# Folding the third hop's weights into the first in a four-layer graph network

## The chip, the cores and the metric

The kernel runs on one core of one Trainium2 chip. The time is that of the device for one execution, in microseconds (us); several runs are taken, and the median is compared. One further execution is recorded by the hardware profiler; its span, from the first to the last recorded instruction, is a little shorter than its time.

The engines are called PE (TensorE, the matrix unit), DVE (VectorE), ACT (ScalarE), POOL (GpSimd) and SP (the sync engine, which here issues nearly all loads). Each works through its own instructions in program order.

## The reference

There are 3327 nodes with 64 features and one weighted adjacency matrix `adj` (3327 x 3327, sparse in content, stored dense, fp32). Four layers follow each other, each with a layernorm and a relu ahead and a residual behind:

```python
h = relu(layernorm(x)); x = x + gated(h)     # 2 gated cells: m = adj @ (h W); GRU-like gates; relu
h = relu(layernorm(x)); x = x + ranked(h)    # w = decay ** rank of each nonzero in its row (last 100); w @ (h W) + b
h = relu(layernorm(x)); x = x + squared(h)   # three times: z = (adj * adj) @ z;  z = z @ W.T + b
h = relu(layernorm(x)); x = x + two_hop(h)   # twice: x = tanh([adj @ x, x] @ W[k])
```

So the adjacency is multiplied eight times with a 3327 x 64 matrix, the eight *hops* 0 to 7. Hops 3, 4 and 5 belong to the third layer. With `S = adj * adj` it computes

```
z1 = S h  W0' + b0;   z2 = S z1 W1' + b1;   z3 = S z2 W2' + b2;   x = x + z3
```

where the multiplication by `S` from the left and by a weight from the right may be done in any order.

## The kernel before

**Data.** The nodes are padded to 3328 = 26 blocks of 128. The node features `xs` stay in on-chip memory as 13 positions x 2 halves `s`. Their outputs are made in four *chunks*: chunks 0, 1 and 2 of three positions (384 columns per half), chunk 3 of four (512). Chunks 0 and 1 are group 0, chunks 2 and 3 group 1 (`GROUPS`). A matmul of a hop (`propagate`, L613) takes the node rows `y[k]` of one block as weights and one adjacency tile as moving data, and adds into an accumulator bank per chunk; half `s` of the columns goes to one half of the array's columns. So a sum holds features on partitions (two halves of 64) and nodes along the row. [...] Each tile (128 rows, one group's columns) is loaded by SP into one of 20 slots and is used by hop k and, some units later, by hop k+1.

**Order.** `units` lists (hop, chunk, tile) in the order of the calls at L1044 to L1052: a pass alone for hop 0 of group 0, then joint passes, in which group 1 does hops 0 and 1, group 0 hops 1 and 2, group 1 hops 2 and 3, and so on, the last alone for hop 7 of group 0. In a joint pass the tiles whose source nodes belong to the other group come first; the tiles of the group's own nodes come last, chunk by chunk, so that a chunk's sum ends before the next chunk's last eight tiles (`sweep=8`). Hop k+1 of the pass then asks for the node rows that hop k has just produced, first those of one chunk, then those of the other. The program is laid out by hand: the order in which Python emits instructions is each engine's order. `run` (L717) goes through the units; it emits loads ahead, masks, squares (`square`, L444: ACT, and every third on DVE when no side work is open), the expansion for hop 2 (`expand`, L490), and the matmuls.

**Side work.** What follows a chunk's sum is a generator, `after_0` to `after_7`, begun when the last matmul of that sum is emitted. Each `yield us` puts off its next part until so many nominal microseconds of streaming matmuls have been emitted (`spend`; 0.86 for 512 columns). So a task's parts are strewn among the other instructions, and its parts on DVE stand in one row with those of the other tasks.

**The pieces concerned.**

- `fold_hops` (L228), some 165 us in, multiplies hop 3's and hop 4's weights of the third layer together, so that hop 3 applies W0W1 at once and hop 4 only adds b1. `product(i, j)` puts `bd[i] bd[j]` into `bd[i]`; `bd[:, 1]`, `[:, 2]` and `[:, 3]` are W0, W1 and W2. `brow` holds biases as rows, `hopcol` as columns.
- `after_3` (L991) evacuates hop 3's sum, multiplies it by the weights on PE (`dense_to_nodes`: this matmul turns features into nodes as well) and adds a bias row on DVE.
- `after_4` (L1003) uses `sums_to_nodes` (L813): ACT copies the sum out of the accumulator with a bias per feature, and DVE turns it into node rows by sixteen 32 x 32-block transposes (L825).
- `after_5` (L1006) evacuates (`evacuate`: DVE for even chunks, L761, ACT for odd), multiplies by W2 on PE, adds the result to `xs` on DVE (`residual`, L865), takes layernorm and relu (L843 to L858, the power of -1/2 on POOL at L854), hands over the rows `y[6]`, and later turns them into features by `transpose_on_vector` (L809, sixteen transposes). b2 was added to `xs` at the end of `after_2` (`add_row`, L871).
- `gru` (L874) ends in cell 0 with two relus, the first half on DVE, the second on ACT; `after_0` (L947) then turns both halves into node rows, for group 1 by DVE transposes (L961).
- `last_sources(g)` (L564) builds the weights of each row's last entry, needed at the end of hop 2: POOL clears half a slot (L570), SP loads two pieces (L574), DVE computes (L576, L580), ACT writes `lastw` (L582), and the slot half is freed, which masks (`make_mask`, L472 and the POOL load L477) may take next.
- `after_7` (L1029) ends with the last residual on DVE (L1037) and the output DMA of the chunk (L1039). For the last hop chunk 1 is split into parts 4 (two positions) and 5 (one), so the outputs come as chunks 2, 3, 0, 4, 5.

Of the kernel before, what the change touches and what calls it, by code (L numbers as in the profile page):

```python
# [9 lines left out]
F32 = mybir.dt.float32  # L10
# [3 lines left out]
ALU = mybir.AluOpType  # L14
# [30 lines left out]
N, D = 3327, 64  # L45
P = 128
# [6 lines left out]
NC = 4  # L53
PARTS = (4, 5)
CWM = 512
GROUPS = [(0, 1), (2, 3)]
# [35 lines left out]
def upper(n):  # L92
    return slice(n * D, (n + 1) * D)
# [3 lines left out]
def kernel(  # L97
# [9 lines left out]
    nc = tc.nc  # L107
# [106 lines left out]
    def product(i, j):  # L214

        n, ps = take()
        mm(ps[:, :P], bd[:, i, :], ident)
        tr = work.tile([P, P], F32, name="t2")
        nc.scalar.copy(tr, ps[:, :P])
        give(n)  # L220
        yield 1.0
        n, ps = take()
        mm(ps[:, :P], tr, bd[:, j, :])
        nc.scalar.copy(bd[:, i, :], ps[:, :P])
        give(n)
        yield 1.0

    def fold_hops():  # L228

        i, ps = take()  # L230
        for n in range(3):
            for h in range(2):
                nc.tensor.matmul(ps[upper(h), n * P:(n + 1) * P], brow[:, n], ident, start=True, stop=True)
        cols = work.tile([P, CWM], F32, name="t2")
        nc.scalar.copy(cols[:, :3 * P], ps[:, :3 * P])
        give(i)
        yield 1.0

        i, ps = take()
        mm(ps[:, :D], cols[:, :P], bd[:, 2, :D])  # L240
        nc.vector.tensor_copy(brow[:, 0], ps[:, :D])
        nc.vector.tensor_copy(hopcol[:, 0:1], cols[:, P:P + 1])
        give(i)
        yield 1.0
        yield from product(1, 2)

    def more_constants():
# [60 lines left out]
    def mm(out, lhsT, rhs, start=True, stop=True):  # L308


        for h in range(2):
            hs = slice(h * D, (h + 1) * D)
            nc.tensor.matmul(out[hs], lhsT[:, hs], rhs, start=start, stop=stop)  # L313
# [21 lines left out]
    def give(i):  # L335
        released[i] = max(released) + 1
        (idle_sums if i < 4 else idle_temps).append(i)

    def nodes(c):

        return feat.tile([P, blocks(c), 2, D], F32, name=f"y{c}")

    def flat(t):
        return t.rearrange("p b s d -> p b (s d)")
# [4 lines left out]
    def xchunk(c):  # L349
        return xs[:, CH[c][0]:CH[c][1]]  # L350
# [16 lines left out]
    def begin(c, task):  # L367
        finish(c)
        tasks[c] = [task, 0.0]
        advance(c)  # L370
# [5 lines left out]
    def later_task(us, task):  # L376
        yield us
        yield from task
# [377 lines left out]
    def evacuate(acc, c, busy=False):  # L756
        m = work.tile([P, CWM], F32, name="t2")[:, :width(c)]
        if c % 2 or busy:
            nc.scalar.copy(m, acc[0][1][:, :width(c)])
        else:  # L760
            nc.vector.tensor_copy(m, acc[0][1][:, :width(c)])  # L761
        give(acc[0][0])
        return m

    def dense_to_nodes(ft, w, c):

        i, ps = take()
        v = view(ps, c)
        for b in range(blocks(c)):
            mm(v[:, b, :], ft[:, b * P:(b + 1) * P], bd[:, w - WL1, :])  # L770
        return i, v

    def stacked_to_nodes(c, w):

        i, ps = take()
        v = view(ps, c)
        for b in range(blocks(c)):
            for s in range(2):
                for n in range(2):
                    nc.tensor.matmul(v[upper(n), b, upper(s)], both[c][:, s, b * P + n * D:b * P + (n + 1) * D], w(s),  # L780
                                     start=True, stop=True)
        return i, v
# [78 lines left out]
    def residual(v, c, relu=False):  # L861
        if relu:
            nc.vector.scalar_tensor_tensor(flat(xchunk(c)), v[1], 0.0, flat(xchunk(c)), op0=ALU.max, op1=ALU.add)
        else:
            nc.vector.tensor_tensor(flat(xchunk(c)), flat(xchunk(c)), v[1], ALU.add)  # L865
        give(v[0])

    def add_row(c, i):

        n = 2 * blocks(c)  # L870
        nc.vector.tensor_tensor(groups(xchunk(c)), groups(xchunk(c)),  # L871
                                brow[:, i:i + 1, :].to_broadcast([P, n, D]), ALU.add)

    def gru(acc, c, bi, bh, cell, pace=1.0):  # L874

        w = width(c)
        evacuate_stacked(acc, c, on_scalar=cell == 0)
        yield 0.8 * pace
        at = dead.popleft()
        r, z, d = (slots[at].rearrange("p s w -> p (s w)")[:, i * CWM:i * CWM + w] for i in range(3))  # L880

        def gate(g):
            i, ps = take()
            for s in range(2):
                nc.tensor.matmul(ps[upper(1 - s), :w], cells[:, cell, s, g, :], both[c][:, s], start=True, stop=True)  # L885
            return i, ps

        for g, v in enumerate((r, z)):
            i, ps = gate(g)
            nc.scalar.activation(v, ps[:, :w], AF.Sigmoid, bias=bsum[:, cell, g:g + 1])  # L890
            give(i)
        nh = None if cell == 0 else gate(2)
        ni = gate(3)
        yield 1.0 * pace
        nc.vector.scalar_tensor_tensor(r, ahead[c] if nh is None else nh[1][:, :w], bcol[:, bh + 2:bh + 3], r,
                                       op0=ALU.add, op1=ALU.mult)
        nc.vector.tensor_tensor(r, r, ni[1][:, :w], ALU.add)
        give(ni[0])
        if nh is not None:
            give(nh[0])  # L900
        else:
            del ahead[c]
            if not any(ch in ahead for ch in GROUPS[c // 2]):
                rooms[c // 2].free()
        yield 1.0 * pace
        nc.scalar.activation(r, r, AF.Tanh, bias=bcol[:, bi + 2:bi + 3])
        yield 0.8 * pace
        for s in range(2):
            u = upper(1 - s)
            nc.vector.tensor_tensor(d[u], both[c][u, s], r[u], ALU.subtract)  # L910
        nc.vector.tensor_tensor(d, d, z, ALU.mult)
        nc.vector.tensor_tensor(d, d, r, ALU.add)
        if cell == 0:
            nc.vector.tensor_scalar(both[c][upper(0), 1], d[upper(0)], 0.0, None, op0=ALU.max)
        yield 2.4 * pace
        if cell == 0:
            nc.scalar.activation(both[c][upper(1), 0], d[upper(1)], AF.Relu)
            yield 1.0 * pace
        return at, d
# [27 lines left out]
    def after_0(c, acc):  # L947
        at, _ = yield from gru(acc, c, BI1, BH1, 0)
        dead.append(at)
        yk = nodes(c)  # L950
        if c in GROUPS[0]:
            i, v = stacked_to_nodes(c, lambda s: ident[:, upper(1 - s)])
            yield 0.8
            nc.vector.tensor_copy(flat(yk), v)
            give(i)
        else:
            for s in range(2):
                v = both[c][upper(1 - s), s].rearrange("p (b q n) -> p b q n", q=4, n=32)
                for f in range(2):
                    for q in range(4):  # L960
                        nc.vector.transpose(yk[q * 32:(q + 1) * 32, :, s, f * 32:(f + 1) * 32],  # L961
                                            v[f * 32:(f + 1) * 32, :, q])
                    yield 0.6
        y[1][c] = yk

    def after_1(c, acc):
# [12 lines left out]
    def after_2(c, acc):  # L979
        m = evacuate(acc, c)  # L980
        yield 1.4
        v = dense_to_nodes(m, WL1, c)
        yield 1.2
        residual(v, c)
        yk = nodes(c)
        yield from layernorm_relu(yk, c, squares_on_scalar=c in GROUPS[0])
        y[3][c] = yk
        yield 15.0
        add_row(c, 2)

    def after_3(c, acc):  # L991
        m = evacuate(acc, c)
# [11 lines left out]
        y[5][c] = yield from sums_to_nodes(acc, c, 0)  # L1004

    def after_5(c, acc):  # L1006
        m = evacuate(acc, c)
        yield 0.8
        v = dense_to_nodes(m, WL2 + 2, c)
        yield 0.8  # L1010
        residual(v, c)
        yk = nodes(c)
        yield from layernorm_relu(yk, c)
        y[6][c] = yk
        yield 8.0
        yield from transpose_on_vector(yk, c)
# [12 lines left out]
    def after_7(c, acc):  # L1029
        evacuate_stacked(acc, c)  # L1030
        yield 1.3
        v = stacked_to_nodes(c, lambda s: w3[:, 1, s])
        t = work.tile([P, 4, 2, D], F32, name="t2")[:, :blocks(c)]
        nc.scalar.activation(flat(t), v[1], AF.Tanh)
        give(v[0])
        yield 0.8
        nc.vector.tensor_tensor(flat(xchunk(c)), flat(xchunk(c)), flat(t), ALU.add)  # L1037
        g0, g1 = CH[c]
        nc.scalar.dma_start(out=out[:, g0:g1], in_=xs[:, g0:g1])  # L1039

    after[:] = [after_0, after_1, after_2, after_3, after_4, after_5, after_6, after_7]

# [20 lines left out]
    begin(2, later_task(4.0, before_0(2)))  # L1063
    begin(3, later_task(10.0, before_0(3)))
    begin(NC + 1, later_task(130.0, last_sources(0)))
    begin(NC + 2, later_task(200.0, last_sources(1)))
    run()
    for c in list(tasks):
        finish(c)
# [39 lines left out]
```

## Time and profile before

| | |
|---|---|
| median of 3 runs | 699.59 us (699.44 to 699.65) |
| profiled execution | 699.51 us, its span 697.6 us |
| PE busy | 680.2 us (97%) |
| DVE busy | 354.5 us (51%) |
| ACT busy | 274.4 us (39%) |
| POOL busy | 79.1 us (11%) |
| adjacency and other HBM reads | 199.45 MB, 287 GB/s over the span |

The profile names an instruction by engine and line of the kernel (L613 is line 613), with the tile that it writes and those that it reads. In lists of waits, `X <- Y: a, n, b` says that X stood idle until Y for `a` us in total, in `n` places, the longest of `b`. In a timeline a row has start, duration, engine, line, operation, and in brackets the idle time of the engine ahead of it and what ended it; neighbours of one kind are joined (`x4`). In the slices each digit is the busy share of a fortieth of the span in tenths. Busy time is an average over stages of different kinds; what an edit is worth has to be read in its own stage.

### The profile page before, as it was taken

The page shows a single profiled execution, that of the slowest core. Times are in us where ns is not written, and L with a number is a line of the kernel's source. Part 1 is how long each engine was busy: PE and PEld are TensorE (multiplying, and loading weights), DVE is VectorE, ACT ScalarE, POOL GpSimd, SP SyncE. Part 2 cuts the span into 40 slices and gives each one's busy share as a digit, 9 for nine tenths or more (in the row PEclk, how much of TensorE's full clock was granted, in tenths as well). Part 3 has the DMA queues.
Part 4 walks back from the last instruction along what each step waited for, and adds up shares of the span by engine and source line. Part 5 has one row for each costly group of instructions (what it writes and reads, how often), then busy time and mean ns, then how long its engine had stood idle before and what let it go on. Part 6 is the DMA issues. An engine that isn't in the chain of part 4 may idle for free.

```text
span 697.6 us, 12581 instructions
## 1 busy us (share of the span) xinstructions
PE 680.2 (97%) x5072; PEld 377.9 (54%) x5072; DVE 354.5 (51%) x772; ACT 274.4 (39%) x426; POOL 79.1 (11%) x114
## 2 busy tenths in 40 slices
PE   6899999999999998999999999999999999999997
PEld 4686667635566785556444444333344444344586
DVE  5946745665997899747442107325271565005101
ACT  1013000403147878888998107722176500000101
POOL 5300000002390423111100000000000000000000
PEclk9999999999999999999999999999999999999999
DMA  9999998099879534783899569954998399918991
GB/s 339 401 401 406 405 406 268 3 359 377 268 246 369 212 126 153 267 276 121 288 382 330 203 222 408 405 217 141 394 367 269 105 402 405 405 59 285 403 403 45
DMA packets 68693, 201.31 MB, mean 289 GB/s; under 512 B 7244, under 2 KB 8372, under 8 KB 68636
## 3 DMA queue, kind: packets, MB, share of 16 engines
q1 hardware_dynamic: 65292, 198.69, 76.5%
q10 hardware_dynamic: 1168, 1.63, 0.7%
q8 instruction: 40, 0.66, 0.4%
q0 software_dynamic: 2176, 0.20, 0.2%
q14 instruction: 17, 0.14, 0.1%
HBM read 199.45 MB, written 0.85 MB: 287 GB/s over the span
## 4 chain that ended last, share of the span: by engine, by line
PE 86%; DVE 8%; DMA 3%; POOL 2%; issue 1%; ACT 1%; ACTq 0%; DVEq 0%; POOLq 0%
PE sum L613 73%; PE temp L313 5%; DMA adj<-in_adjT 2%; PE temp L548 2%; PE temp L885 2%; DVE adj L472 2%; PE sum L313 1%; PE sum L885 1%; PE temp L780 1%; DVE e L527 1%; DVE adj L910 1%; POOL both L251 1%; DVE y L961 1%; POOL st L854 1%; DVE st L851 1%
## 5 line engine op out<-in xcount | busy, mean ns | idle before, releaser
L613 PE MATMUL sum<-adj,y 128*64 128x384 f32 (+3 forms) x3016 | 535.5, 501 | 4.0 <-DVE y L858 1.4
L613 PEld LDWEIGHTS sum<-adj,y 128*64 128x64 f32 x3016 | 248.0, 137 | 233.8 <-issue 197.9
L446 ACT ACTIVATE adj<-adj 128x768 f32<-128x768 f32 (+1 forms) x176 | 144.3, 892 | 45.7 <-PE sum L613 21.9
L472 DVE TENSOR_SCALAR adj<-adj 128x768 bf16<-128x768 f32 (+3 forms) x208 | 113.4, 596 | 32.6 <-PE temp L548 24.7
L613 PE MATMUL sum<-e,both 128*64 128x384 bf16 (+1 forms) x624 | 73.9, 339 | 1.1 <-DVE e L527 1.1
L529 ACT ACTIVATE e<-temp,bitsb 128x384 int16<-128x384 f32 (+1 forms) x120 | 67.6, 608 | 14.7 <-PE temp L313 9.4
L830 ACT COPY both<-sum 64x384 f32<-64x384 f32 (+3 forms) x17 | 8.1, 478 | 149.0 <-PE sum L613 147.9
L854 POOL TENSOR_TENSOR st<-st,mhalf 128x6 f32<-128x6 f32 (+1 forms) x16 | 24.9, 1554 | 288.7 <-DVE st L852 288.7
L834 DVE COPY both<-sum 64x384 f32<-64x384 f32 (+3 forms) x13 | 7.2, 560 | 98.6 <-ACT both L830 98.6
L448 DVE TENSOR_TENSOR adj<-adj 128x768 f32<-128x768 f32 (+1 forms) x32 | 30.6, 1005 | 51.8 <-DMA adj<-in_adjT 33.1
L613 PEld LDWEIGHTS <-both 128*64 128x64 bf16 x624 | 41.2, 110 | 19.6 <-issue 7.0
L313 PE MATMUL temp<-adj,tri 128*64 128x384 bf16 (+1 forms) x332 | 51.4, 341 | 0.4 <-DVE e L527 0.2
L477 POOL DMA_DIRECT2D adj<-totals x52 | 34.8, 671 | 46.3 <-PE temp L313 32.4
L527 DVE TENSOR_SCALAR e<-temp 128x384 int16<-128x384 f32 (+1 forms) x46 | 28.3, 616 | 20.6 <-ACT e L529 10.9
L313 PEld LDWEIGHTS <-tri 128*64 128x64 bf16 x416 | 28.9, 110 | 16.1 <-issue 7.8
L809 DVE STREAM_TRANSPOSE both<-y 32x96 f32<-32x96 f32 (+1 forms) x128 | 35.6, 278 | 2.9
L548 PE MATMUL temp<-adj,behind 128*64 128x384 bf16 x208 | 33.8, 340 | 2.6 <-DVE adj L472 2.5
L825 DVE STREAM_TRANSPOSE y<-t 32x96 f32<-32x96 f32 (+1 forms) x64 | 17.8, 278 | 24.7 <-ACT t L816 23.9
L548 PEld LDWEIGHTS <-behind 128*64 128x64 bf16 x208 | 20.8, 110 | 17.2 <-issue 13.3
L761 DVE COPY t<-sum 128x384 f32<-128x384 f32 x6 | 3.3, 553 | 35.8 <-PE sum L613 35.8
L186 ACT COPY t<-temp 128x128 f32<-128x128 f32 x1 | 0.3, 266 | 48.2 <-PE temp L184 48.2
L570 POOL MEMSET adj<- 128x768 f32 (+1 forms) x2 | 1.6, 790 | 139.4 <-PE sum L613 133.9
(132 smaller groups left out, 352.0 us busy)
## 6 DMA issues: line engine op xcount, KB each, us to landing
adj<-in_adjT SPq DMA_DIRECT2D x130, 768.0 KB, 9.1
adj<-in_adjT SPq DMA_DIRECT2D x104, 896.0 KB, 11.6
xs<-in_x ACTq DMA_DIRECT2D x1, 448.0 KB
adj<-totals POOLq DMA_DIRECT2D x26, 3.0 KB, 4.9
adj<-totals POOLq DMA_DIRECT2D x26, 3.5 KB, 2.5
out<-xs ACTq DMA_DIRECT2D x2, 192.0 KB, 4.4
out<-xs ACTq DMA_DIRECT2D x1, 256.0 KB
xs<-in_x ACTq DMA_DIRECT2D x1, 192.0 KB, 3.4
```

Source lines behind the costliest of these rows:

```text
L313: nc.tensor.matmul(out[hs], lhsT[:, hs], rhs, start=start, stop=stop)
L446: nc.scalar.activation(sq, v, AF.Square)
L448: nc.vector.tensor_tensor(sq, v, v, ALU.mult)
L472: nc.vector.tensor_scalar(t.mask.view[:rows, half], t.view()[:rows, half], 0.0, None, op0=ALU.not_equal)
L477: nc.gpsimd.dma_start(out=t.mask.view[P - 1:P], in_=totals[t.g][t.q:t.q + D + 1:D, :])
L527: nc.vector.tensor_scalar(wide[:, s], ps[:, :w], BITS, 0.0, op0=ALU.add, op1=ALU.max)
L529: nc.scalar.activation(wide[:, s], ps[:, :w], AF.Relu, bias=bitsb)
L548: nc.tensor.matmul(counts[c][1][s * D:(s + 1) * D, :w], behind[:, NQ - 1 - t.q:NQ - 1 - t.q + D], t.mask.view[:, s, t.cols(c)], start=firs ...
L613: nc.tensor.matmul(acc[h][1][h * D:(h + 1) * D, :w], yq[h], rhs[h], start=first and n == 0, stop=last and n == len(terms) - 1)
L809: nc.vector.transpose(to[at:at + 32, :, q], h[q * 32:(q + 1) * 32, :, s, f * 32:(f + 1) * 32])
L854: nc.gpsimd.tensor_tensor(st[:, 3, :n], st[:, 2, :n], mhalf[:, :n], ALU.pow)
L885: nc.tensor.matmul(ps[upper(1 - s), :w], cells[:, cell, s, g, :], both[c][:, s], start=True, stop=True)
```

## The change

Six edits:

1. W2 is multiplied into hop 3's weights too: `bd[:, 1]` becomes W0W1W2. The biases follow: `brow[:, 0]` becomes b0W1W2, `hopcol[:, 0]` b1W2 and `hopcol[:, 1]` b2.
2. `after_5` has no matmul any more. It uses `sums_to_nodes` with b2 as ACT's bias, so that DVE turns the sum, and then adds the rows to `xs`.
3. `after_2` no longer adds b2 to `xs`.
4. In cell 0, group 1's first half is turned right after its relu on DVE, inside `gru`; the second half after the relu on ACT; the pauses between the transposes are gone.
5. `last_sources(1)` is due at 240 nominal us instead of 200.
6. The outputs of chunks 0, 4 and 5 are issued on SP's queue instead of ACT's.

```diff
@@ fold_hops
         mm(ps[:, :D], cols[:, :P], bd[:, 2, :D])
+        mm(ps[:, D:D + 1], bd[:, 3, :], cols[:, P:P + 1])
         nc.vector.tensor_copy(brow[:, 0], ps[:, :D])
-        nc.vector.tensor_copy(hopcol[:, 0:1], cols[:, P:P + 1])
+        nc.vector.tensor_copy(hopcol[:, 0:1], ps[:, D:D + 1])
+        nc.vector.tensor_copy(hopcol[:, 1:2], cols[:, 2 * P:2 * P + 1])
         give(i)
         yield 1.0
+        i, ps = take()
+        for h in range(2):
+            nc.tensor.matmul(ps[upper(h), :P], brow[:, 0], ident, start=True, stop=True)
+        col = work.tile([P, P], F32, name="t2")
+        nc.scalar.copy(col, ps[:, :P])
+        give(i)
+        yield 1.0
+        i, ps = take()
+        mm(ps[:, :D], col, bd[:, 3, :D])
+        nc.vector.tensor_copy(brow[:, 0], ps[:, :D])
+        give(i)
+        yield 1.0
+        yield from product(2, 3)
         yield from product(1, 2)
@@ new helper ahead of gru
+    turned = {}
+
+    def turn(yk, c, s):
+        v = both[c][upper(1 - s), s].rearrange("p (b q n) -> p b q n", q=4, n=32)
+        for f in range(2):
+            for q in range(4):
+                nc.vector.transpose(yk[q * 32:(q + 1) * 32, :, s, f * 32:(f + 1) * 32], v[f * 32:(f + 1) * 32, :, q])
@@ gru
             nc.vector.tensor_scalar(both[c][upper(0), 1], d[upper(0)], 0.0, None, op0=ALU.max)
+            if c in GROUPS[1]:
+                turned[c] = nodes(c)
+                turn(turned[c], c, 1)
         yield 2.4 * pace
@@ after_0
-        yk = nodes(c)
         if c in GROUPS[0]:
+            yk = nodes(c)
...
         else:
-            for s in range(2):
-                v = both[c][upper(1 - s), s].rearrange("p (b q n) -> p b q n", q=4, n=32)
-                for f in range(2):
-                    for q in range(4):
-                        nc.vector.transpose(yk[q * 32:(q + 1) * 32, :, s, f * 32:(f + 1) * 32],
-                                            v[f * 32:(f + 1) * 32, :, q])
-                    yield 0.6
+            yk = turned.pop(c)
+            turn(yk, c, 0)
@@ after_2
         y[3][c] = yk
-        yield 15.0
-        add_row(c, 2)
@@ after_5
-        m = evacuate(acc, c)
-        yield 0.8
-        v = dense_to_nodes(m, WL2 + 2, c)
-        yield 0.8
-        residual(v, c)
-        yk = nodes(c)
+        yk = yield from sums_to_nodes(acc, c, 1)
+        nc.vector.tensor_tensor(flat(xchunk(c)), flat(xchunk(c)), flat(yk), ALU.add)
         yield from layernorm_relu(yk, c)
@@ after_7
-        nc.scalar.dma_start(out=out[:, g0:g1], in_=xs[:, g0:g1])
+        queue = nc.scalar if c in GROUPS[1] else nc.sync
+        queue.dma_start(out=out[:, g0:g1], in_=xs[:, g0:g1])
@@ the begins
-    begin(NC + 2, later_task(200.0, last_sources(1)))
+    begin(NC + 2, later_task(240.0, last_sources(1)))
```

## The prediction

> **What bounds the kernel now.** I read the page's engine row and slices first, then TensorE's waits, then timelines around each wait and around the places that the change touches.
>
> The page, engines and the TensorE slices:
>
> ```profile
> PE 680.2 (97%) x5072; PEld 377.9 (54%) x5072; DVE 354.5 (51%) x772; ACT 274.4 (39%) x426; POOL 79.1 (11%) x114
> ...
> PE   6899999999999998999999999999999999999997
> ```
>
> TensorE (PE) is busy for 680.2 of 697.6 us and has no gap from about 340 to 650. The other engines have spare time on average, so only two things count: matmuls added or removed, and anything that makes PE wait. Its waits (total, times, longest):
>
> ```profile
> PE temp L548 <- DVE adj L472: 2.5, 4, 1.3
> PE sum L613 <- DVE e L527: 2.3, 3, 1.2
> PE sum L613 <- DVE y L858: 1.4, 2, 0.9
> PE sum L613 <- DVE y L961: 0.7, 1, 0.7
> ...
> PE temp L313 <- DVE adj L912: 0.3, 1, 0.3
> ```
>
> Nothing here names the third hop of layer 2 (hop 5): its hand-over costs PE only its dense matmuls. VectorE (DVE) there, chunk 0, whose sum ends at 547.46:
>
> ```profile
> 547.48 0.56 DVE L761 COPY t<-sum 128x384 f32<-128x384 f32 x1 [0.70 <-PE sum L613]
> 549.43 0.55 DVE L865 TENSOR_TENSOR xs<-xs,temp 128x384 f32<-128x384 f32 x1 [1.39 <-PE temp L313]
> ...
> 557.10 0.55 DVE L858 SCALAR_TENSOR_TENSOR y<-t,st 128x384 f32<-128x384 f32 x1
> ```
>
> Copy, dense, residual, layernorm: the new node rows y6[0] are ready at 557.65 and PE reads them at 558.88. The slack is 1.2 us. What turns features into nodes costs, groups by form (busy, mean ns):
>
> ```profile
> L809 DVE STREAM_TRANSPOSE both<-y 32x96 f32<-32x96 f32 x96 | 25.9, 270 | 2.5
> L825 DVE STREAM_TRANSPOSE y<-t 32x96 f32<-32x96 f32 x48 | 12.9, 270 | 22.1 <-ACT t L816 21.4
> L313 PE MATMUL temp<-bd,t 128*64 128x128 f32 x148 | 10.2, 273 | 0.0
> ```
>
> Where the first `last_sources(1)` lies (timeline near 278), ScalarE (ACT) near 318, and ACT at the end:
>
> ```profile
> 277.07 1.08 DVE L580 SCALAR_TENSOR_TENSOR adj<-totals,adj 128x896 f32<-128x896 bf16 x1
> 278.19 1.04 ACT L582 ACTIVATE lastw<-adj,bitsb 128x896 int16<-128x896 f32 x1 [0.25 <-DVE adj L580]
> 279.21 1.08 PE L613 MATMUL sum<-adj,y 128*64 128x512 f32 x4 [1.19 <-DVE e L527]
> 279.52 1.40 POOL L477 DMA_DIRECT2D adj<-totals  x1 [5.95 <-ACT lastw L582]
> ```
>
> ```profile
> 317.64 6.42 ACT L529 ACTIVATE e<-temp,bitsb 128x384 int16<-128x384 f32 x13 [0.19 <-PE temp L313]
> ```
>
> ```profile
> 691.34 0.34 ACTq L1039 DMA_DIRECT2D out<-xs  x1
> 691.72 0.76 ACT L830 COPY both<-sum 64x256 f32<-64x256 f32 x2 [1.00 <-DVE xs L1037]
> 694.53 0.28 ACT L1034 ACTIVATE t<-temp 128x128 f32<-128x128 f32 x1 [0.93 <-DVE xs L1037]
> ```
>
> In turn: a long DVE instruction ahead of PE's 1.19 us wait; ACT with no gap for 6.4 us; an output DMA that holds ACT until DVE's last add.
>
> **What the skill says.** "VectorE: DVE Perf Modes", Rules for kernel authors, says that a 32x32 transpose is fastest on DVE. That is true of one block. A chunk of three node blocks here takes 16 such instructions at 284 ns from start to start (the 12.9 us group, with its gaps), 4.54 us, against 0.65 us for the dense step on PE, which multiplies and turns at once. The same table advises fewer DVE operations in a chain; the chain in question grows, and I go by that row. "Perfetto Trace Analysis", Optimizing DMA Performance, Optimization Strategies, wants the matmul engine kept busy by shortening whatever blocks it. The trace agrees: 97% busy, and the cost below comes only from lengthening what PE asks for.
>
> **The change, part by part**, against the profiled execution (span 697.6; 699.51 in all, so 1.9 around it; 0.08 under the median).
>
> (1) First hop's transposes (near 146). The half of chunk 2 that comes from DVE's own relu is turned right after it: 8 instructions, 2.25 us, into DVE's free 133.1-136.1. After ScalarE's relu only 8 remain, not 16. The 0.72 us wait on L961 goes: -0.72. Nothing is late behind it, PE has the operands of the next tile.
>
> (2) Weight folding (163-180). PE gains three small products (0.43) and one more `product` (0.44 from L313's 0.22 a pair of 64x128): +0.87. The 0.31 wait on L912 at 179.74 is covered by the later arrival: -0.31. New ACT copies lie beside over 1.3 us of stream matmuls each. Net +0.56.
>
> (3) Last sources leave 274-279. L580's 1.08 us is no longer ahead of the two L527, so the 1.19 wait falls to about 0.15: -1.04. L576's removal gains nothing, since the L527 after it waits for PE. The removed bias adds (0.6 to 0.7 us each, at 282-293) lie where DVE waits anyway; taking them gains nothing.
>
> (4) They arrive at 305-323. All that it issues moves: the POOL memset, two SP loads, L576, L580, L582. The SP pair waits for the memset and holds four group-1 loads queued behind it; they still land by 313-316, before use near 320. L582 (1.04) enters the gapless stretch of 13 L529, each of which frees the bank that PE's next L313 takes, with no slack at 320.1 and 321.6: about +0.95. The last tile's mask waits for the slot half that L582 frees: ACT end to mask landed was 2.7 us near 279, so ready at 322.5-323.4 against a need near 322.5: 0 to 0.85. I take +1.3 of a bracket 0.5 to 2.3.
>
> (5) Hop 5, chunks 2 and 3. Dense removed: 0.65 + 0.87 = 1.52. In its place the sum of chunk 2, ended at 497.76, goes ACT 498.37, 16 transposes 502.9, add and statistics, four transposes of chunk 3 in between, 508.1; POOL's power until 509.6, but DVE first does 12 more transposes at 316 ns (3.8), so y6[2] is ready near 512.5. PE would be there at 510.9. Wait 1.6; net +0.1. Chunk 3 is ready near 519, wanted near 527.
>
> (6) Hop 5, chunks 0 and 1. Dense removed: 2 x 0.65 = 1.31, so PE would ask for y6[0] at 558.88 - 1.31 = 557.57. The chain: ACT copy 0.58 after a running square, 548.30; 16 transposes 4.54 to 552.87; add 0.59, L843 0.59, L844 0.2, L845 0.6 to 554.85; eight transposes of chunk 1 (2.3) to 557.15, since the order puts them there; L850, L851, L852 1.38 to 558.53; POOL 1.47 to 560.0, chunk 1's other eight transposes to 560.82; L858 0.59 to 561.41. Wait 3.84; net +2.53. Then the order puts the 16 L809 transposes of chunk 0 (4.7) ahead of chunk 1's add: 566.1; add and statistics 1.98 + 1.38, POOL 1.47, L858 0.6: 571.5. PE wants y6[1] twelve matmul pairs of 0.645 after y6[0], 561.41 + 7.74 = 569.15: wait 2.35. The evacuation L834 of chunk 1 behind another 16 transposes: about +0.6. Sum +5.5, bracket 5 to 6; I carry +5.6. In before both were free.
>
> (7) End. Without its DMA issue ahead, ACT copies (L830) from about 691.0 and does the last tanh about 1.2 earlier; SP is free by then. Last DMA issue 695.16 to about 694.0: -1.2, bracket -0.4 to -1.35.
>
> Squares that fall from ACT to DVE near 342-357 end before L761 needs DVE at 349.7: nothing. Rotation of accumulator banks at 188-230 is not shown: +-0.5, taken as 0.
>
> Sum: -0.72 + 0.56 - 1.04 + 1.3 + 0.1 + 5.6 - 1.2 = +4.6. Profiled 704.1, likewise beside the median (704.2).
>
> **The rivals.** Faster: y6 is ready when PE asks. Its place is 557.57, its price the 3.84 + 1.6 + 2.35 + 0.6 of waits: 704.1 - 8.4 = 695.7. It decides if the chain from sum to y6[0] takes 10.1 us rather than 13.95. For it: DVE is only half busy; against: DVE works it in program order, with 32 transposes ahead of y6[0] (two chunks) and 16 more ahead of y6[1]. About the same: only y6[0] is late, chunk 1 catches up (-2.35 - 0.6) and (4) is free (-1.3): 699.9. Against: sixteen L809 stand ahead of chunk 1 in program order. Slower still: (4) reaches further, since PE and ACT there run in lockstep and DVE's masks and four loads are late with it, 2.5 more: 706.6. For it: the wait on L472 is already 2.5 us. That the change doesn't do what it says: (1) or (3) move their waits rather than end them, +1.7: 705.8; inside the forecast's own range.
>
> **How the numbers follow.** Forecast 704.1, own range 702 to 706.3 (0.60); slower still 0.17; about the same 0.11; faster 0.12. A measurement tells 0.2%, 1.4 us, from no change. The half of "about the same" that ends above 701 counts as slower, so faster 0.12, same 0.07, slower 0.81. Leaving out the faster case and the lower part of "about the same" below, and a few hundredths above, the range is 700.8 to 707.5.
>
> **What would show it.** Right: two new waits of L613 on L858 near 557 and 569, 3 to 4 and 2 to 3 us, one of about 1.6 near 511; no wait on L961; the wait on L527 near 279 mostly gone; L313 or L548 waits of about 1 near 320; the last DMA issue 1.2 nearer to PE's end. Wrong: hop 5's waits under 1 us in all, which makes it faster; or over 3 us near 320, which puts it above the range.

## The result

The changed kernel takes 703.88 us (703.82 to 703.93), the kernel before 699.59. The ratio is 1.0061, with a 95% interval of 1.0048 to 1.0075: slower by 4.3 us. The forecast was 704.1, in a range of 700.8 to 707.5.

The page of the changed kernel, engines and the TensorE slices (lines behind `fold_hops` have moved by 15 or more: L613 is now L628, L858 is L873, L825 is L840, L809 is L824, L313 is L328):

```profile
PE 682.6 (97%) x5040; PEld 374.7 (53%) x5040; DVE 375.8 (54%) x838; ACT 271.4 (39%) x425; POOL 77.6 (11%) x114
...
PE   7899999999999999999999999999999899999997
```

PE executes 32 matmuls fewer and is nevertheless busy for 2.4 us more, of which 1.7 are lost at a low clock, told of below; one slice at the place of hop 5's end has fallen from 9 to 8. DVE has gained 21 us. PE's waits, in total, times, longest:

```profile
PE sum L628 <- DVE y L873: 5.2, 4, 3.3
...
PE temp L563 <- DVE adj L487: 2.6, 4, 1.3
PE temp L328 <- ACT e L544: 0.8, 2, 0.6
PE sum L628 <- DVE e L542: 0.6, 2, 0.5
PE sum L628 <- ACT e L544: 0.5, 1, 0.5
```

The waits on the expansions (L542) fell from 2.3 to 0.6, that on hop 0's transposes is gone, and in their place stand 5.2 us of waits on layernorm's last step, for 1.4 before. Of these 4.6 are for the rows `y[6]`: 1.08 for chunk 2, 3.25 and 0.30 for chunks 0 and 1. PE at the end of hop 5, chunks 0 and 1:

```profile
556.74 1.46 PE L628 MATMUL sum<-adj,y 128*64 128x384 f32 x8
561.45 9.65 PE L628 MATMUL sum<-adj,y 128*64 128x384 f32 x48 [3.25 <-DVE y L873]
571.40 1.83 PE L628 MATMUL sum<-adj,y 128*64 128x384 f32 x10 [0.30 <-DVE y L873]
```

and DVE, which both waits name:

```profile
548.49 4.52 DVE L840 STREAM_TRANSPOSE y<-t 32x96 f32<-32x96 f32 x16 [1.54 <-ACT t L831]
553.04 0.56 DVE L1028 TENSOR_TENSOR xs<-xs,y 128x384 f32<-128x384 f32 x1
...
554.90 2.24 DVE L840 STREAM_TRANSPOSE y<-t 32x96 f32<-32x96 f32 x8
557.17 0.56 DVE L865 TENSOR_TENSOR y<-t 128x384 f32<-128x384 f32 x1
...
558.55 2.25 DVE L840 STREAM_TRANSPOSE y<-t 32x96 f32<-32x96 f32 x8
560.84 0.56 DVE L873 SCALAR_TENSOR_TENSOR y<-t,st 128x384 f32<-128x384 f32 x1
561.43 4.51 DVE L824 STREAM_TRANSPOSE both<-y 32x96 f32<-32x96 f32 x16
565.96 0.56 DVE L1028 TENSOR_TENSOR xs<-xs,y 128x384 f32<-128x384 f32 x1
...
570.78 0.56 DVE L873 SCALAR_TENSOR_TENSOR y<-t,st 128x384 f32<-128x384 f32 x1 [1.50 <-POOL st L869]
```

DVE is the chain here: it never pauses from 548.5 to 569. Chunk 0's rows end at 561.40 (predicted 561.41), chunk 1's at 571.34 (predicted 571.5). The prediction's split into two waits did not come: the 48 matmuls after the first wait take 9.65 us, and only 0.30 of a second wait is left.

To follow where the time goes, I put the start of each streaming matmul of one trace beside the same matmul of the other. The lag of the changed kernel behind the kernel before, at the points where it moves:

| stage | step of the lag | forecast |
|---|---|---|
| hop 0's rows, 146 us | -0.85 | -0.72 |
| folding of weights, 163 to 180 | +0.47 | +0.56 |
| hop 2, at 201 | +0.6 | 0 |
| hop 2, 274 to 279 | -1.56 | -1.04 |
| hop 2, 318 to 323 | +1.44 | +1.3 |
| end of hop 5, chunks 2 and 3 | +0.05 | +0.1 |
| end of hop 5, chunks 0 and 1, to 577 | +5.2 | +5.6 |
| after PE's last streaming matmul | -0.9 | -1.2 |
| sum | +4.4 | +4.6 |

### The profile page after: what moved, and what is told of

Its sections match the earlier page's. It is cut to its first block, busy times and chain, and to the rows that moved or that the text cites. A ratio compares the mean times of both kernels' runs of the same rounds, so it can differ in the third digit from the quotient of the medians.

```text
span 702.0 us, 12591 instructions
## 1 busy us (share of the span) xinstructions
PE 682.6 (97%) x5040; PEld 374.7 (53%) x5040; DVE 375.8 (54%) x838; ACT 271.4 (39%) x425; POOL 77.6 (11%) x114
## 4 chain that ended last, share of the span: by engine, by line
PE 53%; DVE 5%; ACT 1%; issue 1%; POOLq 0%; POOL 0%; DVEq 0%; ACTq 0%
PE sum L628 50%; PE temp L328 2%; DVE y L840 2%; DVE both L824 1%; PE temp L795 1%; DVE y L865 0%; DVE y L873 0%; DVE st L866 0%; ACT e L544 0%; DVE both L849 0%; DVE t L860 0%; DVE st L858 0%; POOL st L869 0%; POOLq L1121 0%; ACT t L831 0%
## 5 line engine op out<-in xcount | busy, mean ns | idle before, releaser
L628 PE MATMUL sum<-adj,y 128*64 128x384 f32 (+3 forms) x3016 | 538.4, 503 | 5.8 <-DVE y L873 5.2
L628 PEld LDWEIGHTS sum<-adj,y 128*64 128x64 f32 x3016 | 245.4, 137 | 242.0 <-issue 202.3
L461 ACT ACTIVATE adj<-adj 128x768 f32<-128x768 f32 (+1 forms) x170 | 139.4, 891 | 26.4 <-DMA adj<-in_adjT 11.9
L628 PE MATMUL sum<-e,both 128*64 128x384 bf16 (+1 forms) x624 | 73.8, 339 | 1.0 <-ACT e L544 0.5
L544 ACT ACTIVATE e<-temp,bitsb 128x384 int16<-128x384 f32 (+1 forms) x120 | 67.9, 607 | 15.3 <-PE temp L328 10.0
L463 DVE TENSOR_TENSOR adj<-adj 128x768 f32<-128x768 f32 (+1 forms) x38 | 36.5, 1009 | 45.7 <-DMA adj<-in_adjT 32.8
L840 DVE STREAM_TRANSPOSE y<-t 32x96 f32<-32x96 f32 (+1 forms) x128 | 35.6, 278 | 42.9 <-ACT t L831 41.1
L328 PE MATMUL temp<-adj,tri 128*64 128x384 bf16 (+1 forms) x332 | 51.5, 341 | 1.3 <-ACT e L544 0.8
L628 PEld LDWEIGHTS <-both 128*64 128x64 bf16 x624 | 41.7, 110 | 19.2 <-issue 7.6
L542 DVE TENSOR_SCALAR e<-temp 128x384 int16<-128x384 f32 (+1 forms) x46 | 28.3, 615 | 20.9 <-PE temp L328 10.1
L328 PEld LDWEIGHTS <-tri 128*64 128x64 bf16 x416 | 28.8, 110 | 17.6 <-issue 10.3
L824 DVE STREAM_TRANSPOSE both<-y 32x96 f32<-32x96 f32 (+1 forms) x128 | 35.6, 278 | 2.3
L831 ACT ACTIVATE t<-sum,hopcol 128x384 f32<-128x384 f32 (+1 forms) x8 | 4.8, 604 | 51.6 <-PE sum L628 51.6
L328 PE MATMUL sum<-adj,tri 128*64 128x384 bf16 (+1 forms) x84 | 15.9, 335 | 0.5 <-DVE e L542 0.4
```

The source lines that it names most:

```text
L461: nc.scalar.activation(sq, v, AF.Square)
L463: nc.vector.tensor_tensor(sq, v, v, ALU.mult)
L542: nc.vector.tensor_scalar(wide[:, s], ps[:, :w], BITS, 0.0, op0=ALU.add, op1=ALU.max)
L544: nc.scalar.activation(wide[:, s], ps[:, :w], AF.Relu, bias=bitsb)
L628: nc.tensor.matmul(acc[h][1][h * D:(h + 1) * D, :w], yq[h], rhs[h], start=first and n == 0, stop=last and n == len(terms) - 1)
L824: nc.vector.transpose(to[at:at + 32, :, q], h[q * 32:(q + 1) * 32, :, s, f * 32:(f + 1) * 32])
```

## Experiments

The theory: hop 5's hand-over costs the whole loss and more, because DVE works it in an order that strings 32 or 48 transposes ahead of rows that PE waits for; the rest of the change about pays for itself or gains. Rivals: the loss sits in other parts; the transposes are too long in any order; the slow matmuls after the wait are a loss of their own.

### One part alone

**Fold alone.** The kernel before with the new `fold_hops`, `after_2` and `after_5` of the diff, in short:

```diff
+        yield from product(2, 3)
         yield from product(1, 2)
@@ after_2
-        yield 15.0
-        add_row(c, 2)
@@ after_5
-        m = evacuate(acc, c)
-        yield 0.8
-        v = dense_to_nodes(m, WL2 + 2, c)
-        yield 0.8
-        residual(v, c)
-        yk = nodes(c)
+        yk = yield from sums_to_nodes(acc, c, 1)
+        nc.vector.tensor_tensor(flat(xchunk(c)), flat(xchunk(c)), flat(yk), ALU.add)
```

> The kernel before, with only the folding of W2, the hand-over of hop 5 by ScalarE and VectorE, and the removed bias additions. Theory (hop 5's hand-over is the loss): +5.2 there, +0.5 to 0.9 in the folding itself, nothing elsewhere: 705.3 (704.8 to 706). Rival (the loss comes from other parts of the change, such as the moved sources): under 702.

Measured 705.96 us, ratio 1.0092 (1.0077 to 1.0107): 6.4 more, so the loss is here and the rival falls. The excess over the 705.3 is the folding's own stage: the lag reaches +0.5 at 181 as forecast, but a new wait of 0.51 on ScalarE's expansion at 202 takes it to +1.1, and it never comes back. The fold takes more accumulator banks, which shifts their rotation; that this is the reason was not tried separately.

**All but the fold.** The changed kernel with that same diff taken back.

> The changed kernel without the folding, the new hand-over of hop 5 and the removed bias additions; what stays is the earlier turning of hop 0's rows, the later sources and the outputs on SP's queue. Theory: 703.9 - 5.2 - 0.5 to 1: 697.9 (697.4 to 698.5), faster than the kernel before. Rival: the parts are not additive, since the removed additions also clear the place that the sources left; then the wait near 276 to 279 stays and it is 699 or more.

Measured 697.63 us, ratio 0.9974 (0.9965 to 0.9984). The parts add up: +6.25 from here to the changed kernel, +6.39 from before to the fold alone. Without the fold, the change would have been a gain of 2 us. The wait at 201 is absent, those at 276 and 279 stay away though the bias additions are back.

**Later sources alone.**

```diff
-    begin(NC + 2, later_task(200.0, last_sources(1)))
+    begin(NC + 2, later_task(240.0, last_sources(1)))
```

> The kernel before, with the last sources of group 1 due at 240 rather than 200. From the two traces: the waits at 276 (0.61) and 279 (1.19) go, and a loss of 1.4 comes at 320 to 323: 699.4 (699.0 to 699.9). If the wait at 276 goes because of the removed bias additions instead, it stays here: 700.0.

Measured 699.56 us, ratio 1.0002 (0.9993 to 1.0011): nothing. Both waits, 0.61 and 1.19, are gone from its trace, and the lag goes from +0.1 to -1.46 and back to -0.02 between 276 and 322. So the bias additions were not the reason for the wait at 276. ScalarE of the changed kernel at the second place:

```profile
317.71 0.57 ACT L544 ACTIVATE e<-temp,bitsb 128x384 int16<-128x384 f32 x1
318.17 1.04 ACT L597 ACTIVATE lastw<-adj,bitsb 128x896 int16<-128x896 f32 x1
319.11 4.05 ACT L544 ACTIVATE e<-temp,bitsb 128x384 int16<-128x384 f32 x8
```

Between expansions that follow one another without a gap stands the 1.04 us step; PE pays for it with waits on L544 (0.16 and 0.61). No wait on a late mask appears.

**Earlier turning alone.** The kernel before with `turn`, `gru` and `after_0` of the diff:

```diff
@@ gru
+            if c in GROUPS[1]:
+                turned[c] = nodes(c)
+                turn(turned[c], c, 1)
@@ after_0, group 1
+            yk = turned.pop(c)
+            turn(yk, c, 0)
```

> The kernel before, with only the earlier turning of hop 0's rows for group 1. Theory: the wait of 0.72 on the last transpose at 146 goes and nothing takes its place: 698.8 (698.6 to 699.1). Rival: what PE gains there it waits for at the next hand-over, 699.6. The new wait of 0.51 on ScalarE's expansion at 201 belongs to the folding's bank rotation, and is absent here.

Measured 698.53 us, ratio 0.9985 (0.9979 to 0.9992): 1.0 less. The wait at 146 is gone and no other came; its lag steps by -0.9 there.

The outputs were not run alone. From the traces: PE's last streaming matmul ends at 692.36 before and at 697.66 after, the last output is issued at 695.16 and at 699.49, 2.80 and 1.83 us later. The last two issues now stand one behind the other on SP, 0.46 us apart.

### The slow matmuls after the wait

Two stretches of the changed kernel: its length, then how long PE, the weight loads, DVE, ACT and POOL were busy in it (with the number of instructions), then the granted TensorE clock as a share of full speed, DMA share, GB/s. The second is the one in which the clock was low, the first the same length ahead of it:

```profile
558.69:562.11 3.42, 0.66 (x4) 0.34 (x6) 3.23 (x12) 0.00 (x0) 1.30 (x1) 1.00 1.02 398
562.11:565.52 3.41, 3.41 (x14) 1.36 (x12) 3.25 (x13) 0.00 (x0) 0.00 (x0) 0.50 1.03 417
```

Soon after the wait PE gets half its clock for 3.41 us, and loses 1.7. Does that cost anything? The second wait, for y6[1], could hide it. Three kernels take the two apart.

**Matmuls in the wait.** The changed kernel with PE kept at work just ahead of y6[0]:

```diff
+            if (k, cs) == (6, 0) and not filled:
+                filled.append(1)
+                i, ps = take()
+                for _ in range(5):
+                    mm(ps[:, :3 * P], ident, bd.rearrange("p a b -> p (a b)")[:, :3 * P])
+                give(i)
             terms = [[yk[:, b - CH[cs][0], s, :]] * 2
```

> The changed kernel, with five pairs of 384-column matmuls on constants (5 x 0.645 = 3.2 us, into an idle bank, read by nobody) put on PE just ahead of the first matmul of hop 6 that reads y6[0]. They fill PE's recorded wait of 3.25 us there. In the trace of the changed kernel PE ran at a clock of 0.53 to 0.62 from 562 to 566, after that wait. Theory A (y6[1] is bound by DVE, so what PE loses after the first wait lies under the second): the clock stays at 1.0, the second wait grows from 0.30 to about 2.2, time unchanged, 703.9 (within 0.3). Theory B (the low clock is a loss of its own): 1.9 less, 702.0. Theory C (the clock doesn't depend on the wait): low clock all the same, 703.9.

Measured 704.00 us, ratio 1.0061 (1.0046 to 1.0076): theory A, no change, and the wait for y6[1] grew to 2.00.

**Chunk 1 not held up.** The sixteen L824 transposes between chunk 0's rows and chunk 1's residual have a plain reason in the code: `propagate` calls `finish(cs)` when rows are missing, and that emits the rest of the task, not only the rows.

```diff
-            if y[k][cs] is None:
-                finish(cs)
+            while y[k][cs] is None:
+                advance(cs)
```

> The changed kernel, with one edit: where a matmul asks for node rows that are not handed over yet, the side task is run on only until they are, not to its end. So the sixteen transposes of chunk 0 into features (4.5 us on DVE) no longer stand ahead of chunk 1's residual. Chunk 1's rows should then be ready near 567, not 571.4. Theory A (DVE's order sets the second wait, the clock is full): y6[1] is read at 561.45 + 7.74 = 569.2, 2.2 less, 701.7. Theory B (low clock after the first wait): PE reaches y6[1] only near 571.1, no wait there, but 0.3 less at most: 703.6.

Measured 703.82 us, ratio 1.0056 (1.0039 to 1.0073): theory B. Chunk 1's rows are now in time (at 566.6) and the second wait is gone, yet nothing is gained, since PE gets there no sooner. The trace is of the slowest of the four executions (704.60): its clock is halved for 6.83 us, from 560.31 to 567.14.

**Both.** The changed kernel with the two diffs above.

> The changed kernel with both edits of the two runs before: constants' matmuls in the first wait, and the side task run on only until its rows are handed over. Theory A and B of the second run differ in what the filler adds to it: under A nothing (701.7 both), under B it brings the 1.9 us of low clock back and only here: near 701.7 against 703.6 without filler.

Measured 701.87 us, ratio 1.0030 (1.0018 to 1.0042), 2.0 less than either. So each edit alone is worth nothing and the two together 2 us: low clock and late rows lie in parallel, and in the changed kernel DVE's chain is the longer by 0.3. PE of this kernel, whose stream starts at the same moment as in the changed kernel (the constants' matmuls lie ahead of it) and runs on without a second wait:

```profile
561.41 11.83 PE L634 MATMUL sum<-adj,y 128*64 128x384 f32 x72
```

The Trainium skill tells of this on the page "TensorE: Matmul & The Clock Gate", What's actually happening: PE goes to half its clock after at least one idle window of about 3.4 us, and that window of 3413 ns runs freely. The traces agree on the length and on the running freely: in each of the 14 kept here, every recorded change of the clock lies a whole number of 3.413 us after the first, and the low clock lasted one such stretch in the changed kernel (3.41 us) and two with chunk 1 not held up (6.83 us). They differ on the idle time: a stretch need not be idle throughout. Two stretches of this grid with chunk 1 not held up, and two of the fold-only kernel, whose recorded wait is 3.25 us as well:

```profile
556.90:560.31 3.41, 1.23 (x8) 0.29 (x4) 3.20 (x11) 0.00 (x0) 1.32 (x1) 1.00 0.97 367
560.31:563.72 3.41, 2.35 (x8) 1.00 (x10) 3.23 (x8) 0.00 (x0) 0.00 (x0) 0.50 1.02 415
```

```profile
557.46:560.87 3.41, 1.76 (x12) 0.55 (x8) 3.20 (x11) 0.00 (x0) 1.19 (x1) 1.00 0.92 329
560.87:564.29 3.42, 1.82 (x12) 0.92 (x14) 3.23 (x12) 0.00 (x0) 0.13 (x1) 1.00 1.02 410
```

Ahead of the two drops PE was idle for 2.76 and 2.18 us of a stretch; in the second kernel 1.06 us of the wait fall into the first low stretch, and another low one follows. In the fold-only kernel the grid cuts the wait into 1.65 and 1.60, and the clock stays full. Its 48 matmuls take 7.96 us, not 9.65, and the second wait is 1.99:

```profile
562.47 7.96 PE L628 MATMUL sum<-adj,y 128*64 128x384 f32 x48 [3.25 <-DVE y L873]
572.41 2.80 PE L628 MATMUL sum<-adj,y 128*64 128x384 f32 x16 [1.99 <-DVE y L873]
```

That is near the split that the prediction had, with the same end.

**Fold alone, chunk 1 not held up.** The fold-only kernel with the edit of `propagate` above (`advance` for `finish`). Here the second wait is no longer a cover.

> The fold-only kernel (705.96) with the side task run on only until its rows are handed over. In its trace PE kept the full clock after the wait of 3.25 us, where the changed kernel dropped to 0.5 after a wait of the same length. If the drop depends on where in time the wait falls, this kernel keeps the clock and gains the 2 us of its second wait: 704.0. If the full clock in that one trace was luck or the drop depends on the work after the wait, it gains at most 0.4, as the changed kernel did: 705.6.

Measured 705.2 us, ratio 1.0079 (1.0062 to 1.0095): neither of the two. In the trace the clock stays full and the span is 2.1 us shorter than that of the fold alone (701.8 against 703.9). Four executions, however, took 703.9, 704.6, 705.8 and 706.9 us, at mean clocks of 0.999, 0.999, 0.997 and 0.995. Those of the fold alone, where DVE's chain covers the drop, took 705.8 to 706.0 at clocks of 0.996 to 1.000. So the drop comes and goes from one execution to the next. (A mean clock of 0.998 alone doesn't show it: some executions of the kernel before have that too, and in its trace the clock drops at 696.47, when PE has no work left.)

**A shorter wait.** One pair of constants' matmuls in place of five, in the kernel with both edits.

```diff
-                for _ in range(5):
+                for _ in range(1):
```

> The kernel with constants' matmuls ahead of y6[0] and the side task run on only until its rows are handed over (701.9), with one pair of those matmuls (0.645 us) instead of five. PE's wait is then about 2.6 us rather than 3.25. If only waits near the length of 3.25 bring the low clock: full clock, 701.9. If 2.6 us are enough: 703.5 or more, or times that scatter between the two as in the fold-only kernel.

Measured 703.1 us, ratio 1.0051 (1.0034 to 1.0068); the recorded wait is 2.60 us. The executions scatter: 701.8 and 702.9 at a mean clock of 1.000, 703.3 and 703.9 at 0.997 and 0.998; their spans fall into two kinds, 699.9 and 699.8 against 701.4 and 701.6. A wait of 2.6 us can be enough too; with it filled, six executions stayed within 701.7 to 702.2. The one trace, of an execution at full clock, has the wait cut by the grid into 1.87 and 0.73.

What decides between a drop and none can be read from the 14 traces together. Of some 2800 stretches of the 3.413 us grid at full clock, none in which PE was idle for up to 1.95 us was followed by a drop (the 1.95 is in the kernel with matmuls in the wait, at 567.94 to 571.35), and each with 2.15 us or more was (the 2.15 is at the end of the kernel at 209 below, at 689.92 to 693.33). So it depends on where the grid falls in the wait, and that differs from one execution to the next: the first change of the clock comes 6.97 to 9.75 us after the start of the 14 traces. An estimate from these figures, with the grid falling anywhere and a limit of 2.05 us: a wait of 3.25 us drops the clock in three executions of four, one of 2.60 in somewhat more than half, one under 1.95, alone in its stretch, in none. This was read off afterwards; no run was made to test it, and the idle times are the recorded ones, with modelled ends of matmuls.

### The order of the transposes

**Transposes held.** The changed kernel with `advance` in place of `finish`, as above, and:

```diff
-    def sums_to_nodes(acc, c, bias):
+    HOLD = {0: 0.8, 1: 3.8, 2: 0.8, 3: 2.4}
+    def sums_to_nodes(acc, c, bias, hold=0.8, pace=1.2):
-        yield 0.8
+        yield hold
-                yield 1.2
+                yield pace
@@ after_5
-        yk = yield from sums_to_nodes(acc, c, 1)
+        yk = yield from sums_to_nodes(acc, c, 1, HOLD[c], 1.8 if c % 2 else 0.9)
-        yield from layernorm_relu(yk, c)
+        yield from layernorm_relu(yk, c, pace=0.9)
-        yield 8.0
+        yield 8.0 if c % 2 else 12.0
```

> The changed kernel with the second run's edit and other pauses: chunks 1 and 3 hold their transposes until the chunk before has gone through its statistics (four of chunk 1's and eight of chunk 3's then stand in the time in which POOL works), and the transposes into features of chunks 0 and 2 come after the rows of chunks 1 and 3. Same arithmetic, same instructions. Theory (the interleaving of two chunks' transposes makes hop 5's rows late, not the transposes as such): y6[0] ready near 556.4 against a need near 557.6, y6[1] near 565.2 against 565.3, y6[2] near 509.5 against 510.9; no wait of a microsecond there, clock full, some 6.3 less than the changed kernel: 697.5 (696.8 to 698.5). Rival (transposes on DVE are too long in any order): waits of 1 to 3 us stay, 700 to 702.

Measured 698.71 us, ratio 0.9986 (0.9980 to 0.9993): 5.2 less than the changed kernel with the same work (DVE 837 instructions for 838, ACT 426 for 425), and faster than the kernel before, though 1.2 slower than expected and outside the range given. The rival falls. DVE of this kernel around chunk 0's rows:

```profile
555.06 0.17 DVE L869 TENSOR_SCALAR st<-st 128x6 f32<-128x6 f32 x1
555.14 1.11 DVE L842 STREAM_TRANSPOSE y<-t 32x96 f32<-32x96 f32 x4
556.74 0.56 DVE L875 SCALAR_TENSOR_TENSOR y<-t,st 128x384 f32<-128x384 f32 x1 [0.49 <-POOL st L871]
```

Four transposes of chunk 1 fit in POOL's time, where the changed kernel puts eight ahead of the variance (L865) and eight more into POOL's time. The rows are ready at 557.3, 4.1 sooner, and PE waits 0.28. For chunk 1 it still waits 0.88 (expected: none), and 0.47 for the evacuation after it. With these and the folding's +1.1, what the dense matmuls saved is spent again: this kernel remains 1.1 above the one without the fold.

### Better than both

The part without the fold, with the sources where neither engine is full and chunk 5's output beside chunk 4's:

```diff
-    begin(NC + 2, later_task(240.0, last_sources(1)))
+    begin(NC + 2, later_task(227.0, last_sources(1)))
@@ after_7
-        queue = nc.scalar if c in GROUPS[1] else nc.sync
+        queue = nc.sync if c in (0, PARTS[0]) else nc.scalar
```

> The changed kernel without the folding (697.63), with the last sources due at 227 and the output of chunk 5 on ScalarE's queue, so that the last two outputs are issued side by side. The sources' last step (1.04 us on ScalarE) then falls near 305, where ScalarE is busy 2.8 of 4 us and not 4.0 of 4: the loss of 1.4 at 320 goes, the waits at 276 and 279 stay away: 697.6 - 1.4 - 0.25 = 696.0. Rival (any place in the hop-2 sweep costs as much): 697.4.

The same with 209 in place of 227:

> The same with the sources due at 209: their steps fall near 284 to 289, where VectorE is busy 2.4 of 4 us and ScalarE 3.4 of 4. If only the stretches before 280 and after 317 are tight: 696.0, as at 227. If the bias additions of before, which stand in this kernel again, leave no room there: 696.5 to 697.5.

At 227: 696.59 us, ratio 0.9955 (0.9942 to 0.9969). At 209: 696.58 us, ratio 0.9953 (0.9940 to 0.9965). Both are 3 us faster than the kernel before, 7.3 than the changed one, and 0.6 short of the 696.0. At 209 the time is that of 227, as its first theory has it, but it also lies in the range of the second, so the two are not told apart. At 227 part of the shortfall lies outside the span: the time around it is 2.3 to 2.5 us in all five executions, for about 2.0 without these two edits, and why isn't shown. In both the waits at 276, 279 and 321 are absent; at 209 one older wait in hop 2 grows from 0.45 to 0.80. The waits of the kernel at 227:

```profile
...
PE temp L548 <- DVE adj L472: 2.4, 4, 1.3
PE sum L613 <- DVE y L858: 0.8, 2, 0.6
PE sum L613 <- DVE e L527: 0.6, 2, 0.5
PE sum L613 <- DMA adj<-in_adjT: 0.6, 2, 0.4
```

## Why the prediction came out right, and where it was off

(1) Right: the wait on hop 0's transposes went and no other took its place. The step measured -0.85, not -0.72.

(2) Right on the products (+0.47 for +0.56). The line "Rotation of accumulator banks at 188-230 is not shown: +-0.5, taken as 0" was the term mis-sized: a new wait at 201, +0.6 in the lag, outside the +-0.5 that it was given.

(3) "L576's removal gains nothing, since the L527 after it waits for PE" was wrong. The wait of 0.61 at 276 went with the moved sources, alone as in the whole change. Measured -1.56 for -1.04.

(4) Right in size, +1.44 for +1.3, and half right in the reason: ScalarE's 1.04 us step did it, the late mask did not show. With (3) the move comes to zero.

(5) Right: +0.05 for +0.1. The dense matmuls' gain of 1.5 us was used up by a wait for y6[2], which PE could read only at 512.55 (forecast 512.5). The recorded wait is 1.08, not 1.6, since PE itself came later than the forecast's 510.9.

(6) Right in its sum and in its two dates, wrong in the split. The first wait was 3.4, not 3.84: PE's next matmul was due at 558.03, not at 557.57 (the constants' matmuls of the kernel with both edits start at 558.00), and came at 561.45. The recorded 3.25 counts only from the modelled end of the last matmul. PE came later in part because its matmuls started 0.36 us apart instead of 0.32 between 550.4 and 552.5, which lost 0.3; no run shows why. The second wait of 2.35 was 0.30, because PE had lost most of it to a lower clock, which the prediction didn't think of: 1.7 at the low clock and 0.5 at the second wait, in the lag. The sum held because it was built from when DVE would be done and not from PE's waits. The evacuation of chunk 1 cost 0.5 of the 0.6 given for it, and 0.1 of the 5.6 was added to the sum of 5.5 without a reason.

(7) The direction was right; -0.9 for -1.2, since outputs 4 and 5 queue on SP one behind the other: with chunk 5's on ACT's queue, at 227, the last issue follows PE's last streaming matmul by 1.58 us and not by 1.83.

The errors of (2), (3), (6) and (7) partly cancel: +0.5, -0.5, -0.4, +0.3. That the forecast fell 0.2 us from the measured time is partly luck; the size and place of the main term are not. Of the signs named ahead, the second wait (2 to 3 us) came as 0.30 and the one near 511 as 1.08 for 1.6; the others came, if not all in their size.

## What to carry to other kernels

Moving a step from the full engine to one that is half idle pays only if the next consumer has slack for the longer chain: 0.65 us of matmul were replaced by 4.5 us of transposes where the slack was 1.2 us. Ask of every new instruction on an in-order engine which rows stand behind it, and look for code that empties a whole task to get at one of its results; most of the loss here was order, and 5.2 us came back with the same instructions. Where two delays lie in parallel, removing one shows nothing: test them singly and together. And a long wait of TensorE can cost more than its length: in these traces one under 1.95 us never brought a low clock, one of 2.6 or 3.25 could cost 2 to 3 us on top.

## What the hardware did that was not expected

A wait of TensorE of 3.25 us, in the middle of a stretch at full clock, was followed in some executions by 3.41 or 6.83 us at half the clock; in others, with the same wait, not. In the traces the clock changes only on a grid of 3.413 us that doesn't start with the wait, and it was halved after each stretch of that grid in which PE had been idle for 2.15 us or more, after none with 1.95 or less. So the drop need not begin when work resumes: it came 0.66 us after that in the changed kernel, and 1.07 us ahead of it with chunk 1 not held up. A wait of 2.6 us left executions that scatter by 2 us in the same way. Where another chain covered the drop, it cost nothing; where none did, the same program varied between 703.9 and 706.9 us.
